# Two attention and expert layers on one core: how the first expert layer's answers are gathered, normalized and handed to the second attention

## The chip, the cores and the metric

One core of a Trainium2 chip runs the whole program. Its engines are TensorE (PE, with its weight loads listed apart as PEld), VectorE (DVE), ScalarE (ACT), GpSimd (POOL) and SyncE (SP); each works off its own queue of instructions in order and waits on semaphores for the others. DMAs are issued from the queues of SP, ACT and POOL and run on 16 shared DMA engines. The metric is device microseconds of one execution; several runs are made, and the median is given.

## What is computed

Eight sequences of 100 tokens with 512 features (800 rows `x`) and a context of 722 rows for each sequence pass through four stages, each added to `x`:

```python
x = x + L0_xattn(layernorm(x), ctx)        # 16 heads of 32, causal
x = x + L0_ffn(layernorm(x))               # 8 experts, top 2, gelu
x = x + L1_xattn(layernorm(x), ctx)        # 16 heads of 64, own keys and context keys
x = x + L1_ffn(layernorm(x))               # 8 experts, top 2, silu
```

The stage that the change touches, and the one behind it, cut to what matters:

```python
def _L0_ffn_ref(x, gamma, beta, Wg, bg, W1, b1, W2, b2):
    xn = (x - mu) / sqrt(var + EPS_LN) * gamma + beta
    probs = softmax(xn @ Wg.T + bg)
    tp, ti = top_k(probs, 2)
    tp = tp / (sum(tp) + 1e-8)
    y = gelu(xn @ W1[e] + b1[e]) @ W2[e] + b2[e]     # for each expert e
    return x + sum over the two chosen e of tp * y

def _L1_xattn_ref(x, memories, ln_g, ln_b, Wq, Wkv, Wm, Wo, bo):
    xn = (x - mu) * rsqrt(var + EPS) * ln_g + ln_b
    q, k, v = heads(xn @ Wq), heads(xn @ Wkv[:, :INNER]), heads(xn @ Wkv[:, INNER:])
    mem = heads(memories @ Wm)
    out = softmax(q @ concat(k, mem).T * scale) @ concat(v, mem)
    return out @ Wo + bo
```

The norm ahead of the attention and the attention's own norm follow each other, so the kernel does both at once (`twice=True`, line 138): one factor per row from one pair of moments.

## The kernel before

All arithmetic is in float32. The 800 rows lie in `x` as seven tiles: the first has 32 rows, the others 128 (`rows`, `starts`). The order of instructions on each engine's queue is set by a scheduler at build time; the program's text fixes what depends on what, and the pools' buffers fix what must come free first.

**Routing.** `Route` (line 219) finds for each row its two experts and the row's place in the table `sent` (`where[0]` for the best expert, `where[1]` for the second), and scatters normalized rows there by indirect DMA from the GpSimd queue. `order` (292) ranks the experts by their number of rows: slot 0 has the most, slot 7 the fewest. `m[0]` and `m[1]` become the two weights.

**The first expert layer** (lines 685 to 732). `work_off` (397) goes through the eight slots. For each, `arrived` (356) loads its rows from `sent` and turns them, `hidden0` (698) multiplies by W1, `products` (366) by W2, and `returned` (386) turns the result back and writes it to the table `answers` in device memory, from the GpSimd queue, in pieces of up to 128 rows. The results of slot k are written while slot k+1 is in `hidden0` (`between`, called after a quarter of it). `rest` (412) is a branch for rows beyond the slots' capacities; with these inputs it isn't taken, but every engine goes through it. At the branch GpSimd waits for all DMAs that it has issued.

**The handover** (lines 734 to 757). `project_early` (467) computes context keys and values of batch 1 for five column blocks (`EARLY[1]`): TensorE multiplies (line 443), ScalarE copies out of PSUM (447), TensorE transposes (455), ScalarE copies (457 to 460), and stores go to `kept_keys` and `kept_values` from the ScalarE queue (465, 475). Then, tile by tile in the text but woven into the former by the scheduler:

- two gathers (`fetch`, 349, 748) from `answers` into the halves of `both`, a tile with two buffers, from the GpSimd queue
- each is weighted and added to `x` on VectorE (749)
- moments (133, 135) on VectorE, the root on ScalarE and a reciprocal on VectorE (`factors`, 151 and 154), the shift (156), and scaling (160) into `xn`, a tile with two buffers
- four transposes on TensorE (171) and four evictions from PSUM on ScalarE with gain and shift (180) into `xT1`
- `bo` is added to `x` on GpSimd (755), for the attention's residual

`bo` itself is loaded on the ScalarE queue (735). After the loop, four 1x1 copies on GpSimd (56, within `weights.load`) that read the last gathered tile open four weight loads on the SP queue (58, `in_Wkv`).

**The second attention** (from 760) begins with the queries: 16 groups of four matmuls (432) from `xT1`, into PSUM tiles with four buffers, evicted by ScalarE (771). Context for its first batch is loaded from the ScalarE queue (877), kept keys and values from the SP queue (781, 465). Their tiles lie where the handover's pools lay, so these loads wait for the last users of that memory. `output` (901) reads `x` again much later.

The root as a power exists already: `factors(..., by_power=True)` (142) computes it with two GpSimd operations, for the norms inside the second attention (911).

Of the kernel before, what the change touches and what calls it, by code (L numbers as in the profile page):

```python
# [13 lines left out]
P = 128  # L14
# [52 lines left out]
def two_layers(ctx: ExitStack, tc: tile.TileContext, a: dict, out: bass.AP):  # L67
# [151 lines left out]
    class Route:  # L219


        def __init__(self, layer, psum, tag):
            self.layer, self.psum, self.tag = layer, psum, tag
            self.logits = routes.tile([P, NTILE, NE], F32, tag="logits", name=f"logits{layer}")
            nc.vector.memset(self.logits, 0.0)
            self.m = [routes.tile([P, NTILE], F32, tag=f"m{k}", name=f"m{k}_{layer}") for k in range(2)]
            self.where = [
                routes.tile([P, NTILE], mybir.dt.int32, tag=f"where{k}", name=f"where{k}_{layer}") for k in range(2)
            ]
            self.sel = routes.tile([P, NTILE, NE], F32, tag="sel", name=f"sel{layer}")  # L230
# [7 lines left out]
        def largest(self, v, m, name):  # L238
# [3 lines left out]
            at = self.temp([P, NTILE, NE], f"at{name}")[:, :g, :]  # L242
# [7 lines left out]
        def group(self, i0, i1, xn, held=()):  # L250
# [3 lines left out]
            at1 = self.largest(v, self.m[0][:, i0:i1], 1)  # L254
            other = self.temp([P, NTILE, NE], "other")[:, :g, :]
            nc.vector.scalar_tensor_tensor(other, at1, -3e38, v, ALU.mult, ALU.add)
            at2 = self.largest(other, self.m[1][:, i0:i1], 2)
# [16 lines left out]
            for k, at in enumerate((at1, at2)):  # L274
                pick = self.temp([P, NTILE, NE], "pick")[:, :g, :]
                nc.vector.tensor_tensor(pick, at, row, ALU.mult)
                place = self.temp([P, NTILE], "place")[:, :g]
# [14 lines left out]
        def order(self, load):  # L292
# [7 lines left out]
            slot = self.temp([P, NE], "slot")  # L300
# [28 lines left out]
            nc.vector.tensor_copy(self.more, most)  # L329

# [66 lines left out]
    def work_off(jobs, arrive, hidden, product, send_back, first=None, midway=None):  # L397
# [5 lines left out]
        for k, (e, r0, n, w1, w2) in enumerate(jobs):  # L403
            h = hidden(e, n, x, w1, lambda: done and send_back(*done))
# [7 lines left out]
    def rest(more, work, first, second, bufs):  # L412

        v = nc.values_load(more[:1, :1], min_val=0, max_val=1)
        with tc.If(v > 0), tc.tile_pool(name="rest", bufs=bufs) as rp:
# [9 lines left out]
            ])  # L425

# [55 lines left out]
    def columns_tile(name):  # L482
        return turned_x.tile([P, DC, NT], F32, tag="xT", name=name)
# [4 lines left out]
    with tc.tile_pool(name="a0", bufs=1) as ap, tc.tile_pool(name="a0w", bufs=3) as aw, tc.tile_pool(  # L488
# [193 lines left out]
        nc.vector.tensor_tensor(m2, m2, s, ALU.mult)  # L682


    with f0, tc.tile_pool(name="f0w", bufs=2) as fw, tc.tile_pool(
# [29 lines left out]
        def work0(jobs, first=None, midway=None):  # L715
# [3 lines left out]
                lambda e, r0, n, yT: returned(0, e, r0, n, yT, fp, ps), first, midway,  # L719
            )  # L720

# [20 lines left out]
        xT1 = columns_tile("xT1")  # L742
        for i in range(NTILE):
            w = rows[i]
            both = fp.tile([P, 2, D], F32, tag="nil", name="back0", bufs=2)
            for k, m in enumerate((m1, m2)):
                y = both[:, k]
                fetch(y, where, i, k)
                nc.vector.scalar_tensor_tensor(
                    x[:w, i, :], y[:w], m[:w, i : i + 1], x[:w, i, :], ALU.mult, ALU.add  # L750
                )
# [3 lines left out]
            nc.gpsimd.tensor_tensor(x[:, i, :], x[:, i, :], bo, ALU.add)  # L755
        weights.limit = len(pieces)
        weights.load(W_L1A + 8, y[:1, :1])
# [349 lines left out]
```

## Time and profile before

| what | us |
|---|---|
| median of 3 runs (1853.73 to 1857.28) | 1853.74 |
| the profiled execution | 1852.47 |
| its span, of which the tables of the profile tell | 1851.0 |
| first expert layer's first hidden matmul | 252.45 |
| last slot's second answers issued | 639.79 |
| first and last gather issued | 646.30, 668.16 |
| last gathered tile added | 673.42 |
| Wkv loads issued from | 674.24 |
| first transposes of `xn` | 675.13 |
| first query matmul | 689.21 |

How to read it: all times are microseconds from the span's start. The page has busy times of the engines, a strip of 40 slices, the DMA queues, the chain of work that ended last (followed back from the end, at each step to what released it), and the costliest groups of instructions. A timeline lists instructions in order of time, equal ones merged, and in brackets how long the engine had been idle before them and what ended that. The granted clock is the share of TensorE's full clock. The page's shares of busy time are means over stages with different limits, so what one stage could give is read in that stage.

### The profile page before, as it was taken

The page shows a single profiled execution, that of the slowest core. Times are in us where ns is not written, and L with a number is a line of the kernel's source. Part 1 is how long each engine was busy: PE and PEld are TensorE (multiplying, and loading weights), DVE is VectorE, ACT ScalarE, POOL GpSimd, SP SyncE. Part 2 cuts the span into 40 slices and gives each one's busy share as a digit, 9 for nine tenths or more (in the row PEclk, how much of TensorE's full clock was granted, in tenths as well). Part 3 has the DMA queues.
Part 4 walks back from the last instruction along what each step waited for, and adds up shares of the span by engine and source line. Part 5 has one row for each costly group of instructions (what it writes and reads, how often), then busy time and mean ns, then how long its engine had stood idle before and what let it go on. Part 6 is the DMA issues. An engine that isn't in the chain of part 4 may idle for free.

```text
span 1851.0 us, 26473 instructions
## 1 busy us (share of the span) xinstructions
PE 1725.6 (93%) x10427; PEld 1305.7 (71%) x10427; DVE 583.7 (32%) x1467; ACT 465.5 (25%) x1390; POOL 159.5 (9%) x266
## 2 busy tenths in 40 slices
PE   4999899999999969999999999999999959999990
PEld 2455578999999835566666656666666649999990
DVE  3464510101111050254454424444344411111115
ACT  2365321111111141343333323333233310010110
POOL 4010210000000040000010000000000010030003
PEclk9999899999999979999999999999999979999995
DMA  9921294454556373031120111213110255565513
GB/s 369 407 78 54 88 343 164 169 193 174 201 199 234 136 256 113 17 97 45 62 71 5 5 35 6 37 10 56 5 6 4 28 201 204 180 218 196 200 62 116
DMA packets 74485, 233.31 MB, mean 126 GB/s; under 512 B 23178, under 2 KB 35582, under 8 KB 57958
## 3 DMA queue, kind: packets, MB, share of 16 engines
q1 hardware_dynamic: 52978, 183.42, 29.0%
q0 software_dynamic: 10048, 30.58, 5.2%
q10 hardware_dynamic: 11316, 17.43, 3.2%
q8 instruction: 86, 1.41, 0.3%
q14 instruction: 57, 0.47, 0.1%
HBM read 180.36 MB, written 51.04 MB: 125 GB/s over the span
## 4 chain that ended last, share of the span: by engine, by line
PE 65%; issue 20%; DMA 10%; DVE 3%; ACT 1%; POOL 0%; POOLq 0%; ACTq 0%; another core or an unknown queue 0%; DVEq 0%
PE ps_m L443 17%; PE ps_col L432 7%; DMA answers<-y 6%; PE ps_sc L808 5%; PE ps_g L989 4%; PE ps_u L989 4%; PE ps_av L858 4%; PE ps_y L374 4%; PE ps_v L890 3%; PE ps_ptA L837 3%; PE ps_o L906 3%; PE ps_mv L455 2%; PE ps_v L535 2%; DMA back<-answers,where 1%; PE ps_o L646 1%
## 5 line engine op out<-in xcount | busy, mean ns | idle before, releaser
L443 PE MATMUL ps_m<-cb,w 128*128 128x361 f32 x896 | 297.3, 482 | 0.0
L374 PE MATMUL ps_y<-h,w 128*128 128x256 f32 (+7 forms) x1536 | 280.5, 344 | 0.0
L374 PEld LDWEIGHTS ps_y<-h,w 128*128 128x128 f32 x1536 | 268.6, 190 | 7.9
L443 PEld LDWEIGHTS ps_m<-cb,w 128*128 128x128 f32 x896 | 169.4, 194 | 102.1 <-issue 14.0
L706 PE MATMUL ps_h<-xgT,w 128*128 128x256 f32 (+7 forms) x1024 | 187.5, 344 | 0.0
L706 PEld LDWEIGHTS ps_h<-xgT,w 128*128 128x128 f32 x1024 | 179.2, 190 | 5.3 <-ACT h L710 0.2
L814 ACT ACTIVATE pr<-ps_sc,m 100x822 f32<-100x822 f32 x128 | 120.0, 943 | 188.1 <-DVE m L812 94.9
L812 DVE TENSOR_REDUCE m<-ps_sc 100x1 f32<-100x822 f32 x128 | 123.8, 1009 | 46.5 <-PE ps_sc L808 46.5
L838 DVE COPY prT<-ps_ptA 128x500 f32<-128x500 f32 x128 | 82.1, 678 | 168.5 <-PE ps_ptA L837 168.5
L447 ACT COPY mT<-ps_m 128x361 f32<-128x361 f32 x128 | 59.0, 462 | 299.2 <-PE ps_m L443 273.8
L710 ACT ACTIVATE h<-ps_h,s_b 128x256 f32<-128x256 f32 (+7 forms) x128 | 56.1, 439 | 303.5 <-PE ps_h L706 303.5
L432 PE MATMUL ps_col<-xT,w 128*128 128x400 f32 x320 | 115.1, 518 | 1.6 <-ACT xT L180 1.6
L989 PE MATMUL ps_g<-xgT,w 128*128 128x256 f32 (+7 forms) x512 | 103.1, 344 | 0.0
L989 PE MATMUL ps_u<-xgT,w 128*128 128x256 f32 (+7 forms) x512 | 102.8, 344 | 0.0
L432 PEld LDWEIGHTS ps_col<-xT,w 128*128 128x128 f32 x320 | 61.9, 197 | 48.0 <-issue 4.5
L808 PE MATMUL ps_sc<-mT,qT 64*100 64x311 f32 (+1 forms) x512 | 93.1, 468 | 0.0
L989 PEld LDWEIGHTS ps_u<-xgT,w 128*128 128x128 f32 x512 | 90.7, 190 | 2.6
L989 PEld LDWEIGHTS ps_g<-xgT,w 128*128 128x128 f32 x512 | 90.5, 191 | 2.7
L858 PEld LDWEIGHTS ps_av<-prT,mv 128*64 128x64 f32 (+1 forms) x1536 | 68.5, 138 | 27.9 <-issue 25.4
L994 ACT ACTIVATE sg<-ps_g 128x256 f32<-128x256 f32 (+7 forms) x64 | 22.3, 349 | 237.6 <-PE ps_g L989 237.5
L858 PE MATMUL ps_av<-prT,mv 128*64 128x100 f32 (+1 forms) x1536 | 81.2, 255 | 0.0
L837 PEld LDWEIGHTS ps_ptA<-ident,pr 100*128 100x128 f32 x640 | 65.2, 140 | 20.7 <-issue 10.6
(250 smaller groups left out, 1821.6 us busy)
## 6 DMA issues: line engine op xcount, KB each, us to landing
w<-in_W SPq DMA_DIRECT2D x64, 1024.0 KB
w<-in_w_gate SPq DMA_DIRECT2D x16, 1024.0 KB
w<-in_w_up SPq DMA_DIRECT2D x16, 1024.0 KB
w<-in_w_down SPq DMA_DIRECT2D x16, 1024.0 KB
sent<-nil SPq DMA_DIRECT2D x25, 512.0 KB
answers<-nil SPq DMA_DIRECT2D x25, 512.0 KB
cb<-in_ctxT ACTq DMA_DIRECT2D x16, 722.0 KB
mT<-kept_keys SPq DMA_DIRECT2D x13, 361.0 KB
```

Source lines behind the costliest of these rows:

```text
L374: nc.tensor.matmul(py[:, k, :n], ws[f // 4][:, f % 4, dc * P : (dc + 1) * P], h[:, f, :n], start=f == 0, stop=f == nf - 1,)
L432: nc.tensor.matmul(ps[:, :HALF], w[c // 4][:, dc, (c % 4) * P : (c % 4 + 1) * P], xT[:, dc, cols], start=dc == 0, stop=dc == DC - 1,)
L443: nc.tensor.matmul(pm[:, : S // 2], w_m[ic // 4][:, dc, (ic % 4) * P : (ic % 4 + 1) * P], cb[h][:, dc, : S // 2], start=dc == 0, stop=dc = ...
L447: nc.scalar.copy(mT[:, h * (S // 2) : (h + 1) * (S // 2)], pm[:, : S // 2])
L706: nc.tensor.matmul(ph[:, :n], w[:, dc, j * P : (j + 1) * P], xg[:, dc, :n], start=dc == 0, stop=dc == DC - 1,)
L808: nc.tensor.matmul(sc[:, bank, c0:c1], qT[r, ic, q0 : q0 + T], keys_, start=True, stop=True)
L812: nc.vector.tensor_reduce(m, sc[:, :, :NKH], AX.XY, ALU.max, negate=True)
L814: nc.scalar.activation(pr.rearrange("p (a n) -> p a n", a=2), sc[:, :, :NKH], AF.Exp, bias=m, accum_out=sums[:, j : j + 1],)
L837: nc.tensor.transpose(pt[:, c, :], pr[:, T + c * P : T + (c + 1) * P], ident[:T, :T])
L838: nc.vector.tensor_copy(prT[:, : NSC - 1, :], pt)
L858: nc.tensor.matmul(po[r, 0, :], vj, prT[j][:w, c, :], start=c == 0, stop=c == NSC)
L989: nc.tensor.matmul(p_[:, :n], w_[:, dc, j * P : (j + 1) * P], xg[:, dc, :n], start=dc == 0, stop=dc == DC - 1,)
```

## The change

Four things are changed, all around the first expert layer.

- After routing, `by_slot` swaps each row's two places and weights so that `where[0]`, `m[0]` belong to the expert with the lower slot, whose answer is made first, and `where[1]`, `m[1]` to the other. For this the places and the one-hot choices are kept in tiles of their own (`self.at`, `self.places`).
- All seven gathers with `where[0]` go out during the last slot (`ahead`, called after slot 6's answers are sent back), into `firsts`: six tiles in the buffer that `xT1` takes later, and the short one in a tile of `b1`'s. If the branch for leftover rows is taken, it fetches them again. After the branch seven operations add them to `x`. The seven gathers with `where[1]` go into `seconds`, seven tiles where the hidden layer lay, after the last slot.
- The roots of this norm are powers on GpSimd; `xn` has four buffers in place of two; the tiles 1, 3 and 5 are evicted from PSUM by VectorE, the others by ScalarE as before.
- `bo` is loaded from the GpSimd queue behind the last scaled tile, and added after that.

```diff
@@ -227,6 +227,10 @@
             self.where = [
                 routes.tile([P, NTILE], mybir.dt.int32, tag=f"where{k}", name=f"where{k}_{layer}") for k in range(2)
             ]
+            self.at, self.places = (
+                [routes.tile(shape, F32, tag=f"{t}{k}", name=f"{t}{k}_{layer}") for k in range(2)]
+                for t, shape in (("at", [P, NTILE, NE]), ("place", [P, NTILE]))
+            )
...
-        def largest(self, v, m, name):
+        def largest(self, v, m, at):
             nc.vector.tensor_reduce(m, v, AX.X, ALU.max)
-            at = self.temp([P, NTILE, NE], f"at{name}")[:, :g, :]
             nc.vector.tensor_tensor(at, v, over_experts(m), ALU.is_equal)
...
-                place = self.temp([P, NTILE], "place")[:, :g]
+                place = self.places[k][:, i0:i1]
                 nc.vector.tensor_reduce(place, pick, AX.X, ALU.add)
                 nc.vector.tensor_copy(self.where[k][:, i0:i1], place)
...
-            slot = self.temp([P, NE], "slot")
+            slot = self.slot = self.temp([P, NE], "slot")
             nc.vector.tensor_reduce(slot, hot, AX.X, ALU.add)
...
 
+        def by_slot(self, behind):
+
+            wide = self.temp([P, NTILE, NE], "pick")
+            nc.gpsimd.tensor_copy(wide[:1, 0, :1], behind[:1, :1])
+            slots = [self.temp([P, NTILE], t) for t in ("key", "mine")]
+            for at, t in zip(self.at, slots):
+                nc.vector.tensor_tensor(wide, at, self.slot.unsqueeze(1).to_broadcast([P, NTILE, NE]), ALU.mult)
+                nc.vector.tensor_reduce(t, wide, AX.X, ALU.add)
+            swap = slots[0]
+            nc.vector.tensor_tensor(swap, slots[0], slots[1], ALU.is_gt)
+            for pair in (self.places, self.m):
+                d = slots[1]
+                nc.vector.tensor_tensor(d, pair[1], pair[0], ALU.subtract)
+                nc.vector.tensor_tensor(d, d, swap, ALU.mult)
+
+                other = self.temp([P, NTILE], "first")
+                nc.vector.tensor_tensor(other, pair[1], d, ALU.subtract)
+                nc.vector.tensor_tensor(pair[0], pair[0], d, ALU.add)
+                nc.vector.tensor_copy(pair[1], other)
+            for k in range(2):
+                nc.vector.tensor_copy(self.where[k], self.places[k])
+
     def rows_of(table, layer, s, r, n):
 
         of_all = table.rearrange("(e r) d -> e r d", e=NE)
@@ -394,14 +419,15 @@
             nc.vector.tensor_copy(y[:w], pt[:w].rearrange("p c d -> p (c d)"))
             nc.gpsimd.dma_start(out=rows_of(answers, layer, e, r0 + s * P, w), in_=y[:w])
 
-    def work_off(jobs, arrive, hidden, product, send_back, first=None, midway=None):
+    def work_off(jobs, arrive, hidden, product, send_back, first=None, midway=None, ahead=None):
 
 
         (x, raw), done = arrive(*jobs[0][:3]), None
         if first is not None:
             weights.load(first + 8, raw[:1, 0, :1])
         for k, (e, r0, n, w1, w2) in enumerate(jobs):
-            h = hidden(e, n, x, w1, lambda: done and send_back(*done))
+            last = k + 1 == len(jobs)
+            h = hidden(e, n, x, w1, lambda: (done and send_back(*done), last and ahead and ahead()))
             if k + 1 < len(jobs):
                 x, raw = arrive(*jobs[k + 1][:3])
             if midway is not None and k == 4:
@@ -409,7 +435,7 @@
             done = e, r0, n, product(e, n, h, w2)
         send_back(*done)
 
-    def rest(more, work, first, second, bufs):
+    def rest(more, work, first, second, bufs, again=lambda: None):
 
         v = nc.values_load(more[:1, :1], min_val=0, max_val=1)
         with tc.If(v > 0), tc.tile_pool(name="rest", bufs=bufs) as rp:
@@ -423,6 +449,7 @@
                 (e, r0, min(CAP, NT - r0), lambda g, e=e: first(piece, e, g), lambda g, e=e: second(piece, e, g))
                 for e in range(NE) for r0 in range(CAPS[e], NT, CAP)
             ])
+            again()
 
     def columns_part(dst, xT, w, h, c, psum, evict):
 
@@ -680,6 +707,7 @@
         nc.vector.reciprocal(s, s)
         nc.vector.tensor_tensor(m1, m1, s, ALU.mult)
         nc.vector.tensor_tensor(m2, m2, s, ALU.mult)
+        route.by_slot(where[1])
 
 
     with f0, tc.tile_pool(name="f0w", bufs=2) as fw, tc.tile_pool(
@@ -712,12 +740,22 @@
                     between()
             return h
 
-        def work0(jobs, first=None, midway=None):
+        def work0(jobs, first=None, midway=None, ahead=None):
             work_off(
                 jobs, lambda e, r0, n: arrived(0, e, r0, n, fw, ps, gamma0, beta0), hidden0,
                 lambda e, n, h, w2: products(n, h, [w2(g) for g in range(NF // 4)], NF, fw, ps, b2s[:, e, :]),
-                lambda e, r0, n, yT: returned(0, e, r0, n, yT, fp, ps), first, midway,
-            )
+                lambda e, r0, n, yT: returned(0, e, r0, n, yT, fp, ps), first, midway, ahead,
+            )
+
+
+        firsts = turned_x.tile([P, NTILE - 1, D], F32, tag="xT", name="firsts")
+        firsts = [firsts[:, i] for i in range(NTILE - 1)]
+        SHORT_AT = rows.index(min(rows))
+        firsts.insert(SHORT_AT, fp.tile([P, D], F32, tag="o_b1", name="first_short"))
+
+        def fetch_firsts():
+            for i in range(NTILE):
+                fetch(firsts[i], where, i, 0)
 
         weights.limit = W_L1A + 4
         work0([
@@ -726,13 +764,15 @@
                 lambda g, k=W_L0F + 8 * e: weights.get(k + 4 + g),
             )
             for e in range(NE)
-        ], W_L0F, fetch_context)
+        ], W_L0F, fetch_context, fetch_firsts)
         rest(
-            more, work0, lambda piece, e, g: piece(of(0, "W1", e, g)), lambda piece, e, g: piece(of(0, "W2", e, g)), 4
+            more, work0, lambda piece, e, g: piece(of(0, "W1", e, g)), lambda piece, e, g: piece(of(0, "W2", e, g)), 4, fetch_firsts,
         )
-
-        bo = fw.tile([P, D], F32, name="bo", bufs=1)
-        nc.scalar.dma_start(out=bo, in_=a["bo"][0].partition_broadcast(P))
+        for i, w in enumerate(rows):
+            nc.vector.scalar_tensor_tensor(
+                x[:w, i, :], firsts[i][:w], m1[:w, i : i + 1], x[:w, i, :], ALU.mult, ALU.add
+            )
+
         for _ in project_early(
             1, [cb[:, h] for h in range(2)], [weights.get(W_L1A + 2 + g, 0) for g in range(2)], lambda: (
                 fw.tile([P, S], F32, tag="xgT", name="mT1"), fw.tile([P, NSC, P], F32, tag="xg", name="mv1")
@@ -740,21 +780,25 @@
         ):
             pass
         xT1 = columns_tile("xT1")
+        seconds = fw.tile([P, NTILE, D], F32, tag="h", name="seconds", bufs=1)
+        for i in range(NTILE):
+            fetch(seconds[:, i], where, i, 1)
         for i in range(NTILE):
             w = rows[i]
-            both = fp.tile([P, 2, D], F32, tag="nil", name="back0", bufs=2)
-            for k, m in enumerate((m1, m2)):
-                y = both[:, k]
-                fetch(y, where, i, k)
-                nc.vector.scalar_tensor_tensor(
-                    x[:w, i, :], y[:w], m[:w, i : i + 1], x[:w, i, :], ALU.mult, ALU.add
-                )
-            xn = fp.tile([P, D], F32, tag="mv", name="xn1", bufs=2)
-            scaled(xn, x[:, i, :], *factors(moments(x[:, i, :], "a1"), "b", twice=True))
-            to_columns(xT1, xn, starts[i], rows[i], ps, gamma1, beta1)
+            nc.vector.scalar_tensor_tensor(
+                x[:w, i, :], seconds[:w, i, :], m2[:w, i : i + 1], x[:w, i, :], ALU.mult, ALU.add
+            )
+            xn = fp.tile([P, D], F32, tag=("mv", "nil")[i % 2], name="xn1", bufs=2)
+            scaled(xn, x[:, i, :], *factors(moments(x[:, i, :], "a1"), "b", twice=True, by_power=True))
+            to_columns(xT1, xn, starts[i], rows[i], ps, gamma1, beta1, vector=i % 2 == 1)
+
+        bo = fw.tile([P, D], F32, name="bo", bufs=1)
+        nc.gpsimd.tensor_copy(bo[:1, :1], xn[:1, :1])
+        nc.gpsimd.dma_start(out=bo, in_=a["bo"][0].partition_broadcast(P))
+        for i in range(NTILE):
             nc.gpsimd.tensor_tensor(x[:, i, :], x[:, i, :], bo, ALU.add)
         weights.limit = len(pieces)
-        weights.load(W_L1A + 8, y[:1, :1])
+        weights.load(W_L1A + 8, seconds[:1, NTILE - 1, :1])
 
 
     with tc.tile_pool(name="a1", bufs=1) as ap, ExitStack() as later, tc.tile_pool(
```

More of the change, by code (lines that the diff above doesn't have):

```diff
@@ L253, in group @@
             g, v = i1 - i0, self.logits[:, i0:i1, :]
[L254 removed]
+            at1 = self.largest(v, self.m[0][:, i0:i1], self.at[0][:, i0:i1, :])
             other = self.temp([P, NTILE, NE], "other")[:, :g, :]
             nc.vector.scalar_tensor_tensor(other, at1, -3e38, v, ALU.mult, ALU.add)
[L257 removed]
+            at2 = self.largest(other, self.m[1][:, i0:i1], self.at[1][:, i0:i1, :])
             short = int(i0 == 0)
```

## The prediction

> **What bounds the kernel now.** I read the page first: its busy shares say that TensorE sets the time almost everywhere.
>
> ```profile
> PE 1725.6 (93%) x10427; PEld 1305.7 (71%) x10427; DVE 583.7 (32%) x1467; ACT 465.5 (25%) x1390; POOL 159.5 (9%) x266
> ```
>
> An edit that removes no matmul can win only where TensorE waits. The change is about the handover from the first expert layer to the second attention, so I took busy times there in stretches of 5 us (columns: PE, PEld, DVE, ACT, POOL, then granted clock, DMA share, GB/s).
>
> ```profile
> 640.00:645.00 5.00, 4.61 (x19) 3.14 (x20) 0.00 (x0) 0.70 (x2) 0.32 (x1) 1.00 0.28 100
> 650.00:655.00 5.00, 1.20 (x6) 0.94 (x7) 4.07 (x7) 1.27 (x4) 3.06 (x4) 0.92 0.67 166
> 655.00:660.00 5.00, 5.00 (x14) 2.75 (x12) 3.31 (x10) 1.18 (x6) 2.78 (x3) 0.74 0.87 274
> 665.00:670.00 5.00, 2.65 (x14) 1.57 (x13) 3.49 (x9) 1.56 (x5) 3.61 (x4) 1.00 0.65 190
> 680.00:685.00 5.00, 1.58 (x7) 1.23 (x8) 3.17 (x9) 3.17 (x11) 1.84 (x2) 0.50 1.02 429
> ```
>
> TensorE is busy 1.20 of 5 us, later 1.58 of 5, and its clock falls to 0.74 and 0.50: this is the hole. The chain of waits (start, us, what) says who digs it:
>
> ```profile
> 601.17 43.68 DMA answers<-y
> ...
> 646.30 3.75 DMA back<-answers,where
> ...
> 667.86 0.29 ACT rb L151
> 668.15 0.36 ACT mT L447
> ...
> 689.21 10.92 PE ps_col L432 x23
> ```
>
> The last expert's answers land at 644.9; gathers follow; ScalarE's root (L151) sits on the path ahead of a copy (L447) that TensorE waits for; the query matmuls (L432) start at 689.21. The timeline shows the waits themselves (start, us, engine, line, then in brackets the idle time before and its cause):
>
> ```profile
> 653.10 0.29 ACT L151 ACTIVATE rb<-mv_a,eps 128x1 f32<-128x1 f32 x1 [4.29 <-DVE mv_a L135]
> 653.80 0.79 PE L455 MATMUL ps_mv<-ident,mT 128*128 128x128 f32 x4 [3.97 <-ACT mT L447]
> 661.41 1.28 POOL L755 TENSOR_TENSOR x<-x,bo 128x512 f32<-128x512 f32 x1
> 661.67 1.58 DVE L749 SCALAR_TENSOR_TENSOR x<-back,m,x 128x512 f32<-128x512 f32 x1 [1.12 <-DMA back<-answers,where]
> 668.16 1.19 POOL L351 DMA_INDIRECT back<-answers,where  x1 [0.30 <-issue]
> 673.52 1.06 POOL L56 COPY w<-back 1x1 f32<-1x1 f32 x4 [2.88 <-PE ps_m L443]
> 681.30 0.56 ACT L151 ACTIVATE rb<-mv_a,eps 128x1 f32<-128x1 f32 x2
> 687.65 1.51 ACT L180 ACTIVATE xT<-ps_tp,p_ln_b,p_ln_g 128x128 f32<-128x128 f32 x4 [0.51 <-PE ps_tp L171]
> ```
>
> The root waits 4.29 us for statistics that wait for gathers, and the next keys' copy stands behind it. A bias add on GpSimd (1.28) stretches VectorE's add beside it from 0.75 to 1.58. Fourteen gathers last until 669.3 because their two buffers must come free.
>
> **The change, part by part.** What starts when was worked out on the built program's order and waits per engine, with durations from these rows. Times are of the profiled execution (1852.47 us, span 1851.0, 1.47 around it); the median of three is 1853.74.
>
> *Swap by slot.* Seventeen VectorE operations (rows of the same kind 0.15 to 0.21 us, some 3.3 us) and one 0.27 us copy on GpSimd, after routing. Two of them rewrite `where` and must wait for the last scatter into `sent`; expert 0's first load waits for it too and went out at 244.05. So the seventeen end by about 245, while VectorE is next wanted at 250.53 (it idled 14.77 us before). GpSimd sits idle 8.80 us there. Cost 0; without that cover at most 3.6.
>
> *Seven gathers during the last expert.* They wait for expert slot 6's answers: second write issued at 607.92, 3.9 us to landing, so 611.9. Seven at the spacing of rows now (0.96 plus 0.30) end at 620.8 and land by 626. The last expert's writes, which now wait for them, go out at 636.29: 10 us of cover. GpSimd has nothing else there. But the seven adds of them to `x` don't start then: in the built program they stand behind the branch for leftover rows, which GpSimd passes only when all its DMAs have landed, 645.2. So 7 x 0.74 = 5.2 us of VectorE lie at 645.2 to 650.4, not at 637.
>
> *Seven gathers instead of fourteen, into seven buffers.* First at 646.3 as now, spacing 1.27, so the last is issued at 653.9 and, 3.75 to 4.5 us from issue start, lands at 657.9 (before: 673.4).
>
> *Roots as powers.* Seven roots and one table load (1.28) leave ScalarE. TensorE's waits for the copies behind them (3.97, 0.45, 2.35, 0.33 in the timeline, 7.1 us) go, and so does the slow clock that followed the first: ten matmul records took 4.80 instead of 3.16. Counted forward from the copy at 647.04, with 16 records in 5.05 us plus transposes (5.7 to 6.0 a unit), the five kept units end at about 667, not 674.7. A power costs two GpSimd steps; the second attention's norms have them: 0.23 and 0.57, and 1.0 us from the end of the statistics to the next VectorE step. Between 0.8 and 1.4 here; I take 1.0.
>
> *What is late next: VectorE with GpSimd's powers.* In the order as built: second adds of tiles 0 and 1 and their statistics to 653.9, tile 2's add to 654.65, wait for the first power until 656.0 (GpSimd is issuing gathers until 654.9), tile 0 scaled by 657.55. The second power is queued behind four copies that open the weight loads (L56, 1.06 us) and wait for the last gather, 657.9; so it ends at 660.3 and VectorE idles 2.8 us. From 660.4, 21 operations to the last statistics: adds 4 x 0.75, statistics 4 x 0.69, aggregates 5 x 0.17, shifts 5 x 0.16, scalings 3 x 0.55, together 9.1, and 0.9 for powers: 670.4. To this I add 0.7: two of the gathers issued beside VectorE's adds lengthened from 0.96 to 1.32, as one now is. 671.1.
>
> [...]
>
> *Turning the tiles.* Scaling tile 4 (0.55) and evicting tile 1 on VectorE (4 x 0.33) end at 673.0. Tile 2's transposes wait for exactly this buffer; then tiles 2, 4 and 6 follow on one bank, each 1.15 from transposes to ScalarE and 1.53 of eviction (rows at 682.84, 683.99, 687.65), 2.75 with the handover: 673.05 + 8.2 = 681.3. Tiles 3 and 5 fit between on VectorE. The queries start at 681.3 instead of 689.2.
>
> *Weight loads 16 us earlier.* Wkv's first load moves from 674.24 to about 659. ScalarE's stores of kept values now take turns on completion counters with them: one waits for the second of these loads, the last unit's for the third. Now the four took 12 us. With the stores beside them (0.72 MB a unit) the third should land at 669 to 671, so ScalarE's first eviction is at about 671, against 673.7 when it is due. Cost 0 up to then, one for one after.
>
> [...]
>
> *Bias later.* Its load waits for the last scaling (674.6), is issued on GpSimd and lands 3.5 later (as `gain` and `bias` do, 3.4 and 3.6; at the start of the kernel such loads took 14 to 16), then 7 adds of 1.27: 688. The context load on ScalarE waits for all seven, and the query evictions stand behind it. TensorE has four PSUM buffers: its first group takes 5.8 at half clock, the others 2.82, so it would stop at 695.5. Cover 7 us. SP's loads of kept keys wait as well; they are wanted at 757 less 8.
>
> *Sum.* 689.2 - 681.3 = 7.9 us, and nothing behind gives it back: from there to the end the same matmuls follow. Span 1843.1; for the median 1853.74 - 7.9 = **1845.8 us**.
>
> **Rivals.** (1) *TensorE alone bounds.* VectorE's waits for powers overlap better than built, and the tiles turn as soon as the kept units end: 667 + 0.4, then two banks at their own pace, 10.3: 677.7. Gain 11.5, 1842.2. For it: waits inferred from semaphores are upper bounds. Against: the second power really stands behind the four copies.
>
> (2) *The hole moves.* ScalarE's stores wait for Wkv, gathers land at the slow end (5.64, as one did), and the kept units still end near 674. Then only the turning is shorter: 7 tiles on two engines, 675.1 + 10.3 = 685.4. Gain 3.8, 1849.9; halved if VectorE is late too, 1851.8. For it: DMA share is 0.82 to 0.87 already at 655 to 665. Against: gathers halve there.
>
> (3) *Slower: the bias in front of the queries.* The context load ahead of the evictions waits for load plus 7 adds. TensorE stops when the bias lands over 10.5 us after issue, and the gain is used up at 18.4 us; at 22 us, 1857.3. For it: the 16.4 us of a like load in the kernel's first stage. Against: DMA is busy there with 400 GB/s, and at 675 Wkv is through.
>
> (4) *It doesn't do what it says.* The first gathers wait for later answers than slot 6's, as the tracking is by whole table: then fourteen gathers remain behind 645 and only buffers and roots win, about 2, 1851.7. Against: the built program's wait is on slot 6's second write.
>
> **How the numbers follow.** Forecast 0.62 (its own range, from the gather's 3.75 to 5.64, the power's 0.8 to 1.4 five times over and the third load's 667 to 675: 1843 to 1848.5), rival 1 0.12, rival 2 0.16, rival 3 0.05, rival 4 0.05. Range 1841.5 to 1851.3: rivals 1 and 2 inside, 3 out. A measurement tells 0.2% here, 3.7 us. Faster by more: 0.62 + 0.12 + half of rival 2 = 0.82; slower 0.05; same 0.13.
>
> **What would show it.** Right: queries start at 680 to 683; no L151 root on ScalarE and no TensorE wait of 2 us or more between 648 and 667; VectorE idles at 657 to 660 behind the four weight copies; Wkv issued at 659. The prediction is wrong if TensorE's last kept unit ends after 670, if a ScalarE store is seen waiting past 672 for Wkv, or if query evictions begin over 14 us after the first query matmul.

## The result, and the profile after

The changed kernel takes 1845.77 us (median of 8 runs, 1839.25 to 1848.16), the kernel before 1853.30 beside it (1849.73 to 1857.28): the ratio is 0.9956, with a 95% interval of 0.9939 to 0.9972, or 5.2 to 11.3 us. The forecast was 1845.8. The profiled execution took 1848.14, its span 1846.2, so it gained 4.8 us of span. The number came out as forecast, and the way to it did not, as the same views show. First the page's busy times and the stretches that were shown of before (PE, PEld, DVE, ACT, POOL, granted clock, DMA share, GB/s).

```profile
PE 1725.2 (93%) x10427; PEld 1306.3 (71%) x10427; DVE 584.5 (32%) x1489; ACT 458.1 (25%) x1370; POOL 167.7 (9%) x283
```

```profile
640.00:645.00 5.00, 4.49 (x19) 3.07 (x20) 0.00 (x0) 0.82 (x2) 0.48 (x1) 1.00 0.27 97
650.00:655.00 5.00, 5.00 (x21) 3.19 (x20) 2.33 (x4) 1.36 (x4) 3.78 (x5) 1.00 0.89 260
655.00:660.00 5.00, 5.00 (x21) 3.16 (x19) 2.35 (x7) 1.51 (x5) 1.63 (x3) 1.00 0.85 275
665.00:670.00 5.00, 0.00 (x0) 0.00 (x0) 4.28 (x11) 0.00 (x0) 1.41 (x3) 0.99 0.96 401
680.00:685.00 5.00, 2.66 (x8) 1.53 (x7) 1.36 (x4) 2.60 (x8) 3.57 (x3) 0.50 0.07 24
```

TensorE now works right through 650 to 660, where it had lost 3.8 us. But from 665 to 670 it and ScalarE do nothing at all, while the DMA engines are 96% busy. The chain of waits (start, us, what) names what moves there:

```profile
619.63 25.50 DMA firsts<-answers,where
654.68 6.43 DMA seconds<-answers,where
661.89 7.96 DMA w<-in_Wkv
672.58 1.69 PE ps_tp L171 x8
683.85 66.27 PE ps_col L459 x192
```

The last gather lands 6.43 us after its issue, at 661.1, and behind it a load of Wkv stands in the chain to the queries. The timeline shows who waits for it (ACTq and SPq are queues issuing DMAs; L492 is the store of kept values, L58 the weight load, L474 the copy out of PSUM, L144 and L145 the power):

```profile
650.52 1.34 POOL L376 DMA_INDIRECT seconds<-answers,where  x1 [0.31 <-issue]
660.98 9.19 ACTq L492 DMA_DIRECT2D kept_values<-mv  x2
661.17 0.54 POOL L56 COPY w<-seconds 1x1 f32<-1x1 f32 x4 [4.37 <-DMA seconds<-answers,where]
661.37 6.43 SPq L58 DMA_DIRECT2D w<-in_Wkv  x4
662.65 0.16 DVE L156 SCALAR_TENSOR_TENSOR tb<-mv_a,rb 128x1 f32<-128x1 f32 x1 [4.55 <-POOL rb L145]
670.27 0.82 ACT L474 COPY mT<-ps_m 128x361 f32<-128x361 f32 x2 [9.16 <-DMA w<-in_Wkv]
670.78 1.54 PE L482 MATMUL ps_mv<-ident,mT 128*128 128x128 f32 x6 [6.14 <-ACT mT L474]
674.29 1.36 DVE L178 TENSOR_SCALAR xT<-ps_tp,p_ln_g,p_ln_b 128x128 f32<-128x128 f32 x4 [0.50 <-PE ps_tp L171]
681.43 8.59 POOL L799 TENSOR_TENSOR x<-x,bo 128x512 f32<-128x512 f32 x7 [2.83 <-DMA bo<-in_bo]
683.85 28.32 PE L459 MATMUL ps_col<-xT,w 128*128 128x400 f32 x79 [1.60 <-ACT xT L180]
```

Read it from ScalarE's side. Two stores of kept values are issued from 660.98; the second takes until 670.2, because in the built program it waits for the second Wkv load to land: both use the same completion counter. (A completion counter is the semaphore on which the built program waits for a DMA's landing; in it this store, of ScalarE's queue, is made to wait for the load that had its counter before, of SyncE's.) The Wkv load goes out behind the four opening copies of 661.17. ScalarE's next copy stands behind the store in its queue (9.16 us idle, by the trace until a Wkv load landed), and the last kept unit's transposes on TensorE behind that copy (6.14). VectorE waits too, 4.55 us for a power that is queued behind the same copies. The queries start at 683.85; before it was 689.21.

The gain does not end there. TensorE's clock is at half from 669.9 (before from 678.1) into the queries. Two stretches of the kernel before, in which its queries start, and two of the changed kernel (same columns):

```profile
688.00:692.00 4.00, 2.79 (x4) 1.50 (x5) 0.00 (x0) 1.16 (x4) 0.00 (x0) 0.50 0.47 122
692.00:696.00 4.00, 4.00 (x9) 2.11 (x8) 0.00 (x0) 0.50 (x1) 0.00 (x0) 0.61 1.04 398
```

```profile
684.00:688.00 4.00, 4.00 (x8) 2.24 (x9) 0.00 (x0) 0.00 (x0) 4.00 (x4) 0.63 0.00 0
688.00:692.00 4.00, 4.00 (x13) 2.25 (x13) 0.00 (x0) 0.99 (x2) 2.02 (x2) 1.00 0.23 53
```

A mean of 0.61 over four us is half clock until 695.1, 5.9 us into the queries; 0.63 is half clock until 687.0, 3.1 us into them. (In stretches of 1 us the clock reads 0.50 up to 695, 0.93 from 695 to 696 and 1.00 from 696 before, and 0.50 up to 686, 0.52 from 686 to 687 and 1.00 from 687 after.) The 2.8 us less at half speed should be worth 1.4, and from the first query to the first value matmul of the next step it took 67.51 us before (689.21 to 756.72) and 66.11 after (683.85 to 749.96). The changed kernel's second profile (e0 below) fits: a mean of 0.65 in 684 to 688 is half clock for 4.5 us of the queries, and the same way took 66.77. So the profile's gain is 5.5 us from the first gather behind the branch to the queries (42.91 to 37.42), and 1.4 by the clock. That is 6.9, and the span is only 4.8 shorter: some 2 us go again behind that value matmul (1094.3 us to the end before, 1096.2 after), in code that the change doesn't touch.

### The profile page after: what moved, and what is told of

The parts are those of the page before. It is cut to its first block, busy times and chain, and to the rows that moved or that the text cites. A ratio compares the mean times of both kernels' runs of the same rounds, so it can differ in the third digit from the quotient of the medians.

```text
span 1846.2 us, 26502 instructions
## 1 busy us (share of the span) xinstructions
PE 1725.2 (93%) x10427; PEld 1306.3 (71%) x10427; DVE 584.5 (32%) x1489; ACT 458.1 (25%) x1370; POOL 167.7 (9%) x283
## 4 chain that ended last, share of the span: by engine, by line
PE 62%; issue 15%; DMA 7%; POOL 1%; DVE 1%; ACT 1%; POOLq 0%; ACTq 0%; another core or an unknown queue 0%; SPq 0%; DVEq 0%
PE ps_m L470 14%; PE ps_h L734 10%; PE ps_y L399 9%; PE ps_sc L852 5%; PE ps_col L459 5%; PE ps_av L902 4%; PE ps_v L934 3%; PE ps_ptA L881 3%; DMA answers<-y 3%; PE ps_o L950 3%; PE ps_mv L482 2%; DMA firsts<-answers,where 1%; DMA back<-answers,where 1%; PE ps_tp L171 1%; ACT pr L858 1%
## 5 line engine op out<-in xcount | busy, mean ns | idle before, releaser
L474 ACT COPY mT<-ps_m 128x361 f32<-128x361 f32 x128 | 58.8, 462 | 311.1 <-PE ps_m L470 276.5
```

Source lines behind the costliest of these rows:

```text
L474: nc.scalar.copy(mT[:, h * (S // 2) : (h + 1) * (S // 2)], pm[:, : S // 2])
```

## The experiments

All were timed beside the kernel before, each set on one chip: e0 to e3 in the first set, e4, e7, e8 and e10 in the second, the others in the third. Below, "handover" is the time from the first gather behind the branch to the first query matmul, read from each profile's timeline; the time is the median. The two profiles of the changed kernel agree in their handover (37.42 and 37.38), and so do the two of e1 (31.16 and 31.47); every other kernel has one profile.

| run | edit | time, us | ratio to before, 95% | handover, us |
|---|---|---|---|---|
| before | | 1854.53, 1853.56, 1852.40 in three sets | | 42.91 |
| e0 | none | 1845.73 | 0.9957 (0.9940 to 0.9973) | 37.38 |
| e1 | Wkv late | 1839.55 | 0.9914 (0.9895 to 0.9934) | 31.16 |
| e1, again | | 1840.76 | 0.9941 (0.9927 to 0.9955) | 31.47 |
| e11 | Wkv by GpSimd's queue | 1841.40 | 0.9938 (0.9924 to 0.9952) | 33.47 |
| e10 | Wkv earlier | 1845.91 | 0.9962 (0.9949 to 0.9975) | 36.34 |
| e2 | roots on ScalarE | 1842.72 | 0.9937 (0.9917 to 0.9957) | 33.91 |
| e7 | Wkv late, roots on ScalarE | 1842.98 | 0.9939 (0.9922 to 0.9955) | 33.88 |
| e4 | before with powers alone | 1851.00 | 0.9988 (0.9980 to 0.9997) | 44.75 |
| e3 | first gathers late | 1851.98 | 0.9981 (0.9969 to 0.9994) | 42.99 |
| e8 | Wkv late, first gathers late | 1848.18 | 0.9968 (0.9955 to 0.9981) | 41.15 |
| e13 | Wkv late, bias as before | 1846.52 | 0.9968 (0.9956 to 0.9980) | 36.58 |
| e12 | Wkv late, ScalarE evicts all | 1840.61 | 0.9934 (0.9920 to 0.9948) | 30.64 |

**The changed kernel again** (e0).

> The changed kernel once more, as the measure for the runs beside it. Both theories: about 1845.8 us, ratio to before near 0.996. The theory of a wait for weight loads adds: the handover of this profile again shows a store of kept values (L492) on ScalarE's queue behind a Wkv load, and where TensorE's wait after it is longer than the 6.14 us of the first profile, the time is longer by that.

1845.73 us. The wait was 6.10 us (6.14 before), and the handover 37.38 (37.42). Yet the two profiles' spans are 1840.0 and 1846.2: the difference lies in untouched code, 4.7 us behind the first query and 1.5 ahead of the first gather, at a mean granted clock of 0.970 against 0.967. On 1725 us of busy TensorE such a step is 5.3 us by estimate. So one profile's span can't settle an effect of 5 us in this kernel; its handover can, and that is why the table has it.

**Wkv late** (e1).

```diff
-        weights.load(W_L1A + 8, seconds[:1, NTILE - 1, :1])
+        weights.load(W_L1A + 8, xn[:1, :1])
```

> One argument is changed: the four Wkv loads open behind the last scaled tile and not behind the last gather, so no store of ScalarE's can wait for one of them, and the four opening copies no longer stand ahead of the second power on GpSimd. Theory (the stores' wait for Wkv stops TensorE 6.14 us, and VectorE's 4.55 us wait for a power stands behind the copies): both waits are gone from the handover, the last kept unit ends at about 667 and not 672.3, the queries start at 678 to 681 and not 683.85, and the time is 3 to 6 us below the changed kernel, 1840 to 1843. Rival (the store is late because the DMA engines are full, with whatever loads): TensorE's wait stays at 4 us or more, the queries start at 683 to 685, the time stays within 1 us of the changed kernel. A second rival (Wkv now comes too late for the keys): the handover is shorter but TensorE waits later for Wkv, time 1845 to 1850.

6.2 us below the changed kernel in the same set, the handover 6.2 us shorter: somewhat more than the theory had (queries at 678 or later, 1840 us or more). Its timeline:

```profile
656.35 0.19 POOL L144 TENSOR_SCALAR rb<-mv_a 128x1 f32<-128x1 f32 x1 [0.37 <-DVE mv_a L135]
659.96 0.67 ACTq L492 DMA_DIRECT2D kept_values<-mv  x2
668.89 1.09 PE L171 MATMUL ps_tp<-ident,xn 128*128 128x128 f32 x8 [2.59 <-DVE xT L178]
670.53 2.09 SPq L58 DMA_DIRECT2D w<-in_Wkv  x4
676.57 15.85 PE L459 MATMUL ps_col<-xT,w 128*128 128x400 f32 x41 [1.60 <-ACT xT L180]
688.30 0.50 ACT L815 ACTIVATE qT<-ps_col 128x400 f32<-128x400 f32 x1 [11.79 <-POOL x L799]
```

The two stores now take 0.67 us and not 9.19, the second power comes 4.4 us earlier (both counted from the first gather, at 645.41 here and at 646.43 in the changed kernel), and the queries start at 676.57. What TensorE still waits for is VectorE's eviction of tile 1 (2.59). That the loads go out 10 us later costs nothing: no wait for Wkv is found anywhere behind. But this run takes away two things at once, the store's wait and the opening copies' place ahead of the second power, and it lightens the DMA engines besides (0.47 and 0.23 busy from 664 to 668 and from 668 to 672, against 0.96 and 1.01 in the changed kernel). The next two runs part them.

> The kernel with late Wkv loads once more, as the measure for the runs beside it: 1838 to 1841.5 again, and 31.2 us from the first gather behind the branch to the first query matmul.

1840.76; in that set before was 1852.40, 2.1 us less than in the first.

**The same loads from another queue** (e11).

```diff
-    def load(self, n, behind=None):
+    def load(self, n, behind=None, queue=None):
...
-            self.nc.sync.dma_start(out=t[:, :, : piece.shape[-1]], in_=piece)
+            (queue or self.nc.sync).dma_start(out=t[:, :, : piece.shape[-1]], in_=piece)
...
-        weights.load(W_L1A + 8, seconds[:1, NTILE - 1, :1])
+        weights.load(W_L1A + 8, seconds[:1, NTILE - 1, :1], nc.gpsimd)
```

> The changed kernel with one difference: the four Wkv loads are issued from GpSimd's queue and not from SyncE's, at the same point, behind the last gather. So they move the same bytes at nearly the same time, but ScalarE's stores of kept values don't take turns with them. GpSimd's four opening copies stay where they were, ahead of the second power, and the powers behind them come in pairs between the loads. Theory (the wait is the turn on completion counters, not the DMA engines' load): ScalarE waits under 2 us for stores, TensorE's 6.1 us wait is gone, the kept units end at 666 to 668; the queries start 33 to 36 us after the first gather, 1841 to 1845, with VectorE and the paired powers as the next bound. Rival (the DMA engines are full): TensorE's wait before the last kept units stays at 4 us or more, 37 us or more, 1845 to 1849.

```profile
660.24 0.67 ACTq L492 DMA_DIRECT2D kept_values<-mv  x2
660.68 0.64 POOL L58 DMA_DIRECT2D w<-in_Wkv  x1
661.92 0.59 POOL L58 DMA_DIRECT2D w<-in_Wkv  x1
664.44 0.66 PE L482 MATMUL ps_mv<-ident,mT 128*128 128x128 f32 x4 [0.33 <-ACT mT L474]
665.71 0.78 ACTq L492 DMA_DIRECT2D kept_values<-mv  x2
671.01 1.97 PE L171 MATMUL ps_tp<-ident,xn 128*128 128x128 f32 x8 [4.43 <-DVE xT L178]
679.15 21.06 PE L459 MATMUL ps_col<-xT,w 128*128 128x400 f32 x55 [1.60 <-ACT xT L180]
```

The same four loads go out at the same point, 660.68 to 666.2, and the pairs of stores beside them take 0.67 and 0.78 us. TensorE's 6.14 is 0.33. The DMA engines were 76 to 100% busy from 660 to 668, so it was the turn on a counter that stopped ScalarE, and neither their load nor the early loads as such. It is worth 3.9 us of handover (37.38 against 33.47). The 2.0 to 2.3 us that are left to e1 (33.47 against 31.47 and 31.16) are VectorE's, with its powers in pairs behind the copies and the loads: TensorE waits 4.43 us for its eviction. The medians of e11 and e1 in this set, 1841.40 and 1840.76, are too close to show them.

**Wkv earlier still** (e10).

```diff
-        weights.load(W_L1A + 8, seconds[:1, NTILE - 1, :1])
+        weights.load(W_L1A + 8, seconds[:1, 0, :1])
```

> The four Wkv loads are opened behind the first of the seven second gathers instead of the last, so the opening copies pass GpSimd as soon as it has issued the gathers, at about 655, and the loads go out some 5 us earlier than in the changed kernel. The stores of kept values still take turns with them. Theory (TensorE's 6.1 us are the time from the store to the landing of the second Wkv load, VectorE's 4.6 us the time that the opening copies wait): VectorE's wait goes and TensorE's shrinks to 1 to 4 us, the queries start 2 to 5 us earlier: 1841 to 1844. Rival (the loads now take DMA share from the gathers, whose landing sets VectorE): gathers land later than 6.9 us after their issue, no gain, 1845 to 1848.

```profile
654.38 1.06 POOL L56 COPY w<-seconds 1x1 f32<-1x1 f32 x4
656.77 0.19 POOL L144 TENSOR_SCALAR rb<-mv_a 128x1 f32<-128x1 f32 x1 [0.38 <-DVE mv_a L135]
666.89 0.82 ACT L474 COPY mT<-ps_m 128x361 f32<-128x361 f32 x2 [6.66 <-DMA w<-in_Wkv]
667.40 1.02 PE L482 MATMUL ps_mv<-ident,mT 128*128 128x128 f32 x6 [3.65 <-ACT mT L474]
670.60 1.68 PE L171 MATMUL ps_tp<-ident,xn 32*128 32x32 f32 x8 [2.18 <-ACT mv L484]
```

The time is the rival's, 1845.91, but not for the rival's reason. VectorE's wait behind the copies is gone, as the theory has it, and the wait of TensorE shrinks to 3.65. Then ScalarE stands a second time, for 2.25 us, and TensorE for 2.18: 5.8 in all. (The trace puts the end of this to the landing of a store of kept values; in the built program the store of kept keys in between waits for the third Wkv load.) The handover is 1.1 us shorter. So VectorE's 4.55 us in the changed kernel were nearly free, since ScalarE and TensorE stood longer.

**Roots back on ScalarE**, with early and with late loads (e2, e7).

```diff
-            scaled(xn, x[:, i, :], *factors(moments(x[:, i, :], "a1"), "b", twice=True, by_power=True))
+            scaled(xn, x[:, i, :], *factors(moments(x[:, i, :], "a1"), "b", twice=True))
```

> The roots of this norm go back to ScalarE, all else as in the changed kernel. The prediction's step says that TensorE's 7.1 us of waits for copies behind the roots come back; in the chain to the queries that is worth 3 to 7 us: 1849 to 1853. Rival (with the gathers early the statistics come early too, so the roots wait for nothing and cost only their 0.3 us each and a table load): within 1.5 us of the changed kernel, 1845 to 1847.

Both missed: the median is 3.0 us lower with the roots (the intervals of the two ratios overlap), and the handover is 3.5 us shorter. With the roots, GpSimd has nothing between the gathers and the opening copies, and TensorE is late with its kept units:

```profile
654.89 0.66 PE L482 MATMUL ps_mv<-ident,mT 128*128 128x128 f32 x4 [1.98 <-ACT mT L474]
657.28 1.88 POOL L56 COPY w<-seconds 1x1 f32<-1x1 f32 x4 [3.08 <-DMA seconds<-answers,where]
657.76 5.76 SPq L58 DMA_DIRECT2D w<-in_Wkv  x4
664.35 1.57 ACTq L492 DMA_DIRECT2D kept_values<-mv  x2
666.30 0.46 ACT L474 COPY mT<-ps_m 128x361 f32<-128x361 f32 x1 [1.83 <-DMA kept_values<-mv]
```

Against the changed kernel's second profile, whose first gather comes at the same time (644.96 and 644.92), the loads go out 2.5 us earlier (660.23 there) and the store arrives 4.8 us later (659.51), so most of its wait is gone. If that is the whole reason, the powers must win once no store waits:

> The late Wkv loads and the roots on ScalarE together. The run with late loads alone (powers kept) took 1839.6, the run with roots alone 1842.7. Theory: with powers the kept units end early, at about 665.5 to 667 when nothing waits for Wkv; roots bring back TensorE's waits for copies, 2 to 4 us of which reach the queries: 1841.5 to 1844. So the powers help where no store waits for a load, and only seemed to cost in the changed kernel because they bring the stores to ScalarE's queue earlier than Wkv lands. Rival (powers cost by themselves, by GpSimd's steps on VectorE's path): faster than with late loads alone, 1836 to 1838.5.

By the handover they do: 33.88 us against 31.16 and 31.47, 2.4 to 2.7 us, and with the roots TensorE waits 5.3 us in all for copies out of PSUM (L474), with the powers 2.2. The medians alone don't settle it: 1842.98, 0.9939 of before, against 0.9914 and 0.9941 for e1 in other sets. With the roots the handovers are alike whenever Wkv is loaded (33.91 and 33.88), with the powers they differ by 6.2 us. That the first two are so alike is partly chance: in e2 14 matmuls from 655.38 took 6.11 us, with weight loads 0.60 us apart from 656.08 to 659.09, and in e7 the same 14 took 4.42, with their 14 weight loads in 3.95. Why the last gather landed by 657.3 with the roots and at 660.0 in that second profile, though issued at the same time, was not tried; the stores of the unit before went out 2.2 us later with the roots, which may be it.

**Powers alone** (e4): the kernel before with the diff above in reverse.

> The kernel before, with nothing but the roots of this norm made powers on GpSimd. The prediction's step (TensorE's 7.1 us of waits for copies behind roots go): the kept units end at about 667 and not 674.7, but the gathers keep their two buffers and the last statistics their 680, so at most 1 to 4 us come through: 1849 to 1853 beside a before of about 1853.5. Rival, from the run with the roots put back, which was 3 us faster than the changed kernel: GpSimd's queue, where powers now stand between gathers and wait for VectorE, makes the later gathers later, so the kernel is slower than before, 1854 to 1858.

The median is 2.6 us lower, within the theory's numbers, but its profile doesn't bear the theory out:

```profile
664.42 14.53 ACTq L465 DMA_DIRECT2D kept_values<-mv  x2
673.97 2.05 SPq L58 DMA_DIRECT2D w<-in_Wkv  x4
679.00 6.78 ACT L180 ACTIVATE xT<-ps_tp,p_ln_b,p_ln_g 128x32 f32<-128x32 f32 x20 [14.45 <-DMA w<-in_Wkv]
```

The kept units do end early, their last stores go out at 664.42, and then the second one waits 14.5 us for a load (the first of Wkv) that is issued only at 673.97. ScalarE's evictions stand behind it, and the handover is 1.8 us longer than before. Where the 2.6 us of the medians come from stays open; the first gather came 2.0 us earlier in this profile than in that of before, in code that the edit doesn't touch.

**First gathers late** (e3, e8).

```diff
-        ], W_L0F, fetch_context, fetch_firsts)
+        ], W_L0F, fetch_context)
...
-            more, work0, lambda piece, e, g: piece(of(0, "W1", e, g)), lambda piece, e, g: piece(of(0, "W2", e, g)), 4, fetch_firsts,
+            more, work0, lambda piece, e, g: piece(of(0, "W1", e, g)), lambda piece, e, g: piece(of(0, "W2", e, g)), 4,
         )
+        fetch_firsts()
```

> The first seven gathers are issued after the branch, directly ahead of the second seven, instead of during the last expert; the rest of the change stays. Theory (gathers set the pace): fourteen in a row at 1.27 end about 8.9 us later, the last lands at about 668 to 670 instead of 661.1, and of this 6 to 8 us reach the queries because ScalarE's wait for Wkv hides part of nothing: 1851 to 1854, next to no gain over before. Rival (ScalarE's and TensorE's chain of kept units up to 672.3 bounds, not the gathers): only the turning moves, 2 to 4 us slower than the changed kernel, 1848 to 1850.

1851.98, and a handover as long as before's (42.99). Here too a store waits for Wkv in the built program (11.26 us, in front of the tiles' evictions), so the run was made again with late loads:

> Fourteen gathers behind the branch again, with the late Wkv loads. With early Wkv loads the early gathers were worth 6.2 us (1851.98 against 1845.73), of which one ScalarE wait for Wkv in front of the tiles' evictions may be a part. Theory (gathers and the adds behind them set the last statistics): 5 to 8 us slower than the run with late loads alone, 1844.5 to 1848. Rival (the worth of early gathers came from where the Wkv wait fell): 1840 to 1843.

```profile
662.46 1.28 POOL L376 DMA_INDIRECT seconds<-answers,where  x1 [0.30 <-issue]
678.42 1.97 PE L171 MATMUL ps_tp<-ident,xn 128*128 128x128 f32 x8 [7.78 <-DVE xT L178]
```

10.0 us of handover (41.15 against 31.16) go when the gathers lie in a row behind the branch: the last one goes out 17.1 us after the first (8.2 in e1), and TensorE waits 7.78 us for an eviction by VectorE (2.59 in e1). The time, 1848.18, is 0.2 above the theory's range and far from the rival's. This is the largest part of the change.

**The bias as before**, with late loads (e13): `bo` loaded on ScalarE's queue, and added tile by tile. The line stands behind the branch, but the scheduler puts the load far ahead: it was issued at 215.2, and at 216.0 in the kernel before.

```diff
+        bo = fw.tile([P, D], F32, name="bo", bufs=1)
+        nc.scalar.dma_start(out=bo, in_=a["bo"][0].partition_broadcast(P))
...
-        bo = fw.tile([P, D], F32, name="bo", bufs=1)
-        nc.gpsimd.tensor_copy(bo[:1, :1], xn[:1, :1])
-        nc.gpsimd.dma_start(out=bo, in_=a["bo"][0].partition_broadcast(P))
-        for i in range(NTILE):
             nc.gpsimd.tensor_tensor(x[:, i, :], x[:, i, :], bo, ALU.add)
```

> Late Wkv loads, with the bias loaded early on ScalarE's queue and added tile by tile on GpSimd as in the kernel before. The prediction puts the bias behind the norm at cost 0, and the adds between at the lengthening of VectorE's adds (0.75 to 1.58) and a longer GpSimd queue ahead of the powers. Theory: seven adds of 1.28 between the powers make the last statistics 2 to 5 us later, 1841 to 1845. Rival (the late bias costs, because query evictions wait 11.7 us for it): faster than with late loads alone, 1836 to 1838.5.

```profile
657.30 1.28 POOL L796 TENSOR_TENSOR x<-x,bo 128x512 f32<-128x512 f32 x1
658.66 0.52 POOL L144 TENSOR_SCALAR rb<-mv_a 128x1 f32<-128x1 f32 x1
672.44 1.97 PE L171 MATMUL ps_tp<-ident,xn 128*128 128x128 f32 x8 [5.85 <-DVE xT L178]
```

Adds stand between the powers on GpSimd, VectorE is late, and TensorE waits 5.85 us for its eviction. The move of the bias is worth 5.1 us of handover (36.58 against 31.47) and 5.8 of time (1846.52 against 1840.76), 1.5 more than the theory's range allowed. Its delay is hidden: in e1 the query evictions begin 11.7 us after the queries, and TensorE doesn't stop.

**ScalarE evicts all tiles**, with late loads (e12): `vector=i % 2 == 1` is left out.

> Late Wkv loads, and all seven tiles evicted from PSUM by ScalarE, none by VectorE. The prediction's step (turning takes 8.2 us because two engines share the evictions): seven evictions in a row, one of 1.18 and six of 1.50, from about 665.9 end at 676.1, so the queries start at about 676.2 to 677.5, within 1 us of the run with late loads. That is, the sharing is worth little once VectorE is itself late with the last norm. Rival (sharing is worth what it takes off ScalarE, 4 us): queries 3 to 4.5 us later, 1842 to 1844.

30.64 us of handover, 0.5 to 0.8 less than with VectorE's share, and the same time. With late loads this part of the change wins nothing.

Each part was left out alone, with the others in. Their worths (10.0, 5.1 and 2.7 us) add up to more than the 11.4 to 11.8 us by which e1's handover is shorter than that before, so they are not independent. The swap by slot and the four buffers of `xn` were not tried by themselves.

## Why the prediction was right, and where it was not

- *Swap by slot* was hidden: its last operation began at 243.19, and the first hidden matmul came at 251.72 (252.45 before). *Seven gathers during the last expert* were issued from 612.0 to 620.6 (forecast 611.9 to 620.8), and their adds began behind the branch at 645.27.
- *Seven gathers instead of fourteen*: last issued at 654.7 (653.9), but landed 6.43 us later, not 3.75 to 4.5: 661.1, not 657.9. The lengthening of the gathers beside VectorE's adds was 0.7 us in all (1.08, 1.10, 0.99 and 1.34 against 0.96), as taken. In the kernel before, a scatter beside a VectorE product of 2.04 us had taken 2.76 against 0.96 (at 231.22); none of the four lost as much.
- *Roots as powers*: TensorE's waits between 648 and 664 went, and two units had a pace of 5.5 us each.
- The step that failed is *Weight loads 16 us earlier*, "Cost 0 up to then, one for one after". The waits were read off correctly from the built program: one store waits for the second load, the last unit's for the third. But only the last unit's was given a price, against the first eviction. It was the other, one unit earlier, that stopped ScalarE at 661, with the last unit's copies still behind it. It cost 6.1 us of TensorE and, by e11, 3.9 us of handover, and the kept units ended at 672.3, not 667. That end is one of the three signs named as refuting, so by its own signs the mechanism was wrong there; the other two (a store waiting past 672, evictions over 14 us after the first query) were not seen. Of the signs for it, the roots left ScalarE and VectorE idled behind the four copies, but TensorE's long wait began at 664.6, before 667, Wkv went out at 661.4 and not at 659, and the queries started at 683.85 and not by 683.
- *The load of the DMA engines* was not what cost: they were 96% busy from 665 to 670, but in e11 they were 76 to 100% busy from 660 to 668 and the pairs of stores took 0.67 and 0.78 us. What cost here was the turn on a counter.
- *What is late next*: VectorE did wait behind the four copies, 4.55 us (forecast 2.8). It cost little, as TensorE was later still (e10); with TensorE's wait gone, VectorE's lateness cost 2.0 to 2.3 us (e11).
- *Turning the tiles*: 8.2 us from the eviction of tile 1 to the queries. It was 8.2, from 675.65 to 683.85; the step began 2.6 us late and so ended 2.5 late.
- *Bias later*: landed 3.4 us after issue (3.5), TensorE didn't stop. The prediction gives the move no gain of its own; by e13 it is worth 5.1 us of handover.
- *Sum*: 7.9 us up to the queries; the profile has 5.5, and 1.4 more by the clock, which the sum had left out. The medians have 7.5, with an interval of 5.2 to 11.3. So the total was right within what a median can tell, but partly by luck: one cost was missed (2.4 us up to the queries) and one gain (1.4), and they nearly made up for each other. The way it went was nearer to rival 2, which had named this wait, late gathers and kept units that end near 674, at a gain of 3.8.

## What to carry to other kernels

When a transfer is moved earlier, ask what else takes turns with it: here a DMA issue waited for the landing of another queue's transfer (9.2 us), even for one that hadn't been issued (14.5 us in e4), and everything behind it on its engine waited too. Go through every such wait that the built program shows, with the time at which the waiting instruction is reached, and price the earliest first. An edit can lose in one surrounding and win in another: the powers cost 3.5 us of handover with early loads and won 2.4 to 2.7 with late ones (the medians don't settle either), so the parts of a change should be tried in the version that has the hindrance removed. The kernel with late Wkv loads is one line from the changed one and beats both: by 6.2 and 15.0 us in the set where all three ran, and by 11.6 the kernel before in the other.

## What the runs showed of the hardware

A second issue on ScalarE's queue stood for 9.2 us (changed kernel) to 14.5 us (e4) on a completion counter that the built program shares out to loads of SyncE's queue too; with the same loads on GpSimd's queue (e11) the stores took 0.67 and 0.78 us. TensorE was granted half its clock for some 17 us, from about 670 to 687 in the changed kernel and from 678 to 695 in that before (stretches of 1 us read 0.50 in between, and at the edges 0.95 and 0.52 in the changed kernel, 0.54 and 0.93 in that before): through the tiles' transposes (in the kernel before from the third tile on) and 3 to 6 us into the queries, although TensorE was busy for 3.26 of the 4 us from 676 to 680 in the changed kernel. And equal code at granted clocks of 0.967 and 0.970 differed by 4.7 us behind the first query.
